# A four-layer scan and attention kernel: the program points at which transfers are issued are moved by a few tiles

## The chip, the cores and the metric

The kernel runs on one core of a Trainium2 chip. The metric is the device time of one launch in microseconds (us), as the median of repeated runs. A profile of one execution is shown beside it. Engines are written as in the profile: PE (matmul) and PEld (its weight loads), DVE (vector), ACT (scalar), POOL (GpSimd), and SP, the engine on which every transfer of this kernel is issued.

## The reference

The input is four images of 64 by 64 pixels and 96 channels. Layers 0 and 1 are state-space layers, layers 2 and 3 are attention without a softmax, each with a quantized feed-forward part:

```
x = x + ssm0(groupnorm(x));  x = x + ssm1(groupnorm(x))
t = tokens(x)
t = t + attn(ln(t));  t = t + ffn8(ln(t))        # layer 2, then the same for layer 3

ssm(x):   xi, z = split(x @ in_proj.T)                       # 192 channels each
          xc = silu(depthwise_conv3x3(xi) + b)
          for k in 0..3:                                     # four scan orders of the 4096 pixels
              dt, B, C = project(xc in order k);  delta = softplus(dt @ w + b)
              h[t] = exp(delta[t] * A) * h[t-1] + delta[t] * xc[t] * B[t]     # 16 states a channel
              y   += (sum over states of h[t] * C[t]) + D * xc,  put back in pixel order
          return (layernorm(y) * silu(z)) @ out_proj.T
```

In layer 0 the orders k = 1 and k = 3 run down the columns of the image. In layer 1 the orders run through windows of 2, 4 and 8 pixels.

## The kernel before, in words

Two images are worked on together: the 128 partitions hold 64 channels of each, and three groups j of 64 channels make the 192. Layers 0 and 1 with two pairs of images give four phases. A phase has 16 blocks, one for each order k and each quarter t of 1024 pixels, so there are 64 blocks. A block has 48 tiles: two halves g of the states, three channel groups j, eight states n. In all there are 3072 tiles, and the main loop walks over them with the index `i`. I call `i` modulo 48 the place in the block.

For tile i, POOL multiplies the state by C (`weigh`, L695). For the five states in `POOL_N` POOL also makes delta·x·B (`begin`, L652), and for the others PE spreads B (`row`, L662) and DVE multiplies (`product`, L676). ACT makes the decay (`decays`, L669), DVE scans (`scan`, L684), and PE sums over the states (`gather`, L727). `begin` runs two tiles ahead of the scan.

What a block needs is brought by transfers:

- The rows of B and C, spread over 64 partitions each, `brep` and `crep` (`rows_of` sets the tile, `spread`, L642, issues two transfers for a row). They share 11 buffers.
- Copies of delta and delta·x (`twice`, L592), four of each for every j, into 12 buffers `dup`. They run across the block boundary, up to place 55, that is place 7 of the next block.
- The next block's x (`load`, L529 and L532, places 1, 2 and 5 for k from 1 to 3), the partial result of this block (`recall`, L704, seven tiles ahead: places 41, 1 and 9), and the store of a finished partial result (`flush`, L744, places 34, 42 and 50, that is 2).
- B and C on their way through memory (`rows`, L555).

The convolution of the next pair (`conv_pieces`) and the closing part of the last pair (`tail_pieces`) are generators. They run in the background: the loop calls `advance()` once for a tile. Three things about it matter here. At 16 places of a block (`kept`: 17 to 32 if the next block has k = 0, else 13 to 28) it isn't called, since `prepare` uses the two `psM` buffers there. What a generator yields says whether it may be left at that point. At the first of the 16 places a generator that yielded something true is driven on within one tile until it yields False:

```
if place == kept[0]:
    while holds:
        advance()
```

A convolution unit (512 pixels) has 32 steps: one before and one after the normalization of its input, and for each j nine taps, each with two matmul calls (L289), and one for z (L299). A unit of the closing part (256 pixels) has 14: two with matmuls into `psM` (L360) and the statistics (L346 to L353), then variance, `normalize`, `back`, `scaled` (L392), two `gate` steps (L398), two output matmuls (L426 to L442), copies and stores.

The orders of PE, DVE, ACT and POOL are the order in which the program is written (`MANUAL`). SP isn't in that set: the framework's scheduler orders its transfers, by the order of writing and by when it believes that what they wait for is done. SP takes its transfers strictly one after the other, and a transfer that waits holds up those behind it.

After the 3072 tiles a planner (`run`) works off the two attention layers and the rest of the closing part.

Of the kernel before, what the change touches and what calls it, by code (L numbers as in the profile page):

```python
# [15 lines left out]
C = 96  # L16
# [6 lines left out]
T = 512  # L23
# [11 lines left out]
def kernel(ctx: ExitStack, tc: tile.TileContext, ins, out, layers=(0, 1, 2, 3)):  # L35
# [176 lines left out]
    def conv_pieces(w, xin, xc, zg, done):  # L212
# [8 lines left out]
        xbs = [part_of(n) for n in range(3)]  # L221
        yield False
        yield False
        for i in range(2):
# [35 lines left out]
        def load(t):  # L260
# [14 lines left out]
            return pads  # L275

        done.append(now[0])
        coming = load(0)
        for t in range(NT):
            pads, coming = coming, None  # L280
            yield False
            for i in range(2):
                nc.scalar.activation(pads[i][1], pads[i][1], AF.Identity, bias=norms[i][1], scale=norms[i][0])  # L283
            yield False
            for j in range(J):
                px = psM([128, T])
                for tap in range(9):
                    for i in range(2):
                        nc.tensor.matmul(  # L289
                            px[64 * i : 64 * i + 64], w["wf"][:, tap, 64 * j : 64 * j + 64],  # L290
                            pads[i][0][:, tap // 3 : tap // 3 + rows, tap % 3 : tap % 3 + HW],
                            start=(tap == 0), stop=(tap == 8),
                        )
                    yield MORE if tap < 8 else True
                xo = thin([128, T], "xo")
                nc.scalar.activation(xo, px, AF.Silu, bias=w["cb"][:, j, :])
                pz = psM([128, T])
                for i in range(2):
                    nc.tensor.matmul(  # L299
                        pz[64 * i : 64 * i + 64], w["wz"][:, 64 * j : 64 * j + 64],  # L300
                        pads[i][0][:, 1 : 1 + rows, 1 : 1 + HW], start=True, stop=True,
                    )
                zo = thin([128, T], "zo")
                nc.scalar.activation(zo, pz, AF.Silu)
                nc.sync.dma_start(xc[:, j, t * T : (t + 1) * T], xo)
                nc.sync.dma_start(zg[:, j, t * T : (t + 1) * T], zo)
                if j == J - 1 and t + 1 < NT:
                    coming = load(t + 1)
                if j == J - 1:
                    done[0] += 1  # L310
                yield False

    def tail_pieces(w, units, y, zg, xin, xout, tokens):
# [11 lines left out]
        for t in units:  # L325
            tt = slice(t * U, (t + 1) * U)
            if coming is None:
                while t * U >= flushed(y):
                    yield False
                coming = load(t)  # L330
                yield False
                yield False
            (yu, zu), coming = coming, None
            yt = wide([128, J, U], "yt")
            yt = yt.rearrange("p j (q c) -> p (j q c)", q=2).rearrange("p (q i j c) -> p q i j c", q=2, i=2, j=J)
            yn = yu.rearrange("p j c -> p (j c)").rearrange("p (q j i c) -> p q j i c", q=2, j=J, i=2)
            xr = st([C, 2, U], F32, "xr", 1)
            for i in range(2):
                nc.sync.dma_start(xr[:, i, :], xin[i][:, tt])

# [58 lines left out]

            normalize(0)  # L400
            yield False
            pn0 = back(0)
# [14 lines left out]
            if tokens:  # L417
# [12 lines left out]
                for i in range(2):  # L430
                    nc.scalar.copy(xo[:, i], pos[i][:, :, 0:C])
                    nc.sync.dma_start(xout[i][tt].rearrange("(q p) c -> p q c", p=128), xo[:, i])
                ready[0] = t + 1
            else:
# [9 lines left out]
                for i in range(2):  # L444
                    nc.scalar.copy(xo[:, i, :], pos[i])
                    nc.sync.dma_start(xout[i][:, tt], xo[:, i, :])
            yield False

# [52 lines left out]
    def prepare(ph, k, t):  # L501
# [47 lines left out]
        def rows(s):  # L549
            if s == 0:  # L550
                p["parts"] = st([96, TB], BF16, "spB", 2)
                p["bc"] = dr.tile([4 * N, TB], F32, tag="bc", name="bc", bufs=2)
            rests.append(thin([76, T], "proj"))
            nc.scalar.copy(rests[s], pps[s])
            nc.sync.dma_start(p["bc"][:, halves[s]], rests[s][0 : 4 * N])  # L555

# [44 lines left out]
        for j in range(J):  # L601
# [9 lines left out]
            at(base + 16 + (3 if k == 0 else 4) * j, inputs, j)  # L611
            copies = max(32 + 8 * j, base + 17)
            for m, key in enumerate(("deltas", "dus")):
# [3 lines left out]
        for s in range(2):  # L617
            at(base + 3 + s, rows, s)
            for q in range(3):
                at(base + 3 + 2 * q + s, cut, s, q)  # L620
# [5 lines left out]
    def rows_of(at, g):  # L626
# [3 lines left out]
        for n in range(g * GN, (g + 1) * GN):  # L630
            for v in (0, 1):
                if v or n in POOL_N:
                    out.append((first + n - g * GN - (7 if v else 9), at, v, n))
        return sorted(out)
# [97 lines left out]
    def flush(i):  # L732
# [9 lines left out]
        for src, dst in made[at]["views"]:  # L742
            nc.scalar.copy(src(yb), dst(py))  # L743
        nc.sync.dma_start(made[at]["img"](yd[ph][:, j, :]), yb)  # L744

# [268 lines left out]
    per = NG * J * GN  # L1014
    made, reps, sums, states, scanned, order = {}, {}, {}, {}, {}, [None]
    end = len(tiles)
    now, rest = [0], (L - TB) // 256
    with tc.manual_schedule(engines=MANUAL):
# [26 lines left out]
        rows = [row for at in range(len(blocks)) for g in range(NG) for row in rows_of(at, g)]  # L1045
        for i in range(-9, end + 4):
            while rows and rows[0][0] <= i:
# [164 lines left out]
```

## Time and profile before

| | |
|---|---|
| median of 3 runs | 11149.57 us (11146.85 to 11173.61) |
| the profiled execution's own time | 11149.85 us |
| its span, first to last instruction | 11148.1 us |
| POOL busy in the span | 10204.6 us (92%) |
| DVE busy in the span | 9926.4 us (89%) |
| multiplications by C (L695) | 3072 of 2354 ns, from 140.3 to 10545.8 us |
| transfers issued on SP's queue, share of 16 engines | 66.1% of the span |

An engine's busy time counts its own instructions, not its waits. A row of the profile gives the line, the engine, the operation, the output and inputs by name, the shapes, the count, the busy time, the mean of one in ns, and the idle time of the engine just before these instructions with what ended it. Block 13 is taken as an example later: its first multiplication L695 is number 624, at 2294.1 us, and block 14 begins at 2463.3 us.

### The profile page before, as it was taken

What the parts mean: (1) busy time and instruction counts of PE and PEld (TensorE: products, weight loads), DVE (VectorE), ACT (ScalarE), POOL (GpSimd) and SP (SyncE); (2) the same over time, 40 slices, a digit from 0 to 9 for tenths busy, and PEclk for the clock granted to TensorE, in tenths of its full rate; (3) what the DMA queues carried; (4) which work ended last, traced back from release to release, by engine and by line L of the source; (5) the groups of instructions that cost most, each with busy time, mean ns of one, the idle gap of its engine ahead of it and who ended that gap; (6) DMA issues with size and microseconds to landing.
All of it is one profiled execution on the core that took longest, in us unless ns stands there. A gap on an engine that the chain in (4) does not pass through costs nothing. (4 is left out here: it accounts for less than half of the span.)

```text
span 11148.1 us, 101994 instructions
## 1 busy us (share of the span) xinstructions
PE 8910.0 (80%) x30112; PEld 2880.5 (26%) x30112; DVE 9926.4 (89%) x6431; ACT 6423.1 (58%) x10575; POOL 10204.6 (92%) x5102
## 2 busy tenths in 40 slices
PE   7978888777777779887788878887778877778777
PEld 2222222111222212221222222222222322222365
DVE  3898999999999889989999999999999999999846
ACT  3656556554566646665566656665466655555576
POOL 3989999999999889999999999999999999999846
PEclk8989999888888889998888889998888888888877
DMA  5679976897578885798666656665556565556410
GB/s 134 158 141 162 141 160 157 145 134 136 149 171 151 140 151 149 157 159 132 138 169 157 157 146 169 164 159 143 149 157 156 155 149 148 143 137 159 122 33 22
DMA packets 1848188, 1604.57 MB, mean 144 GB/s; under 512 B 1412298, under 2 KB 1482892, under 8 KB 1847628
## 3 DMA queue, kind: packets, MB, share of 16 engines
q1 hardware_dynamic: 1847628, 1598.04, 66.1%
q8 instruction: 237, 3.88, 0.2%
q14 instruction: 323, 2.65, 0.1%
HBM read 1008.37 MB, written 186.65 MB: 107 GB/s over the span
## 5 line engine op out<-in xcount | busy, mean ns | idle before, releaser
L695 POOL TENSOR_TENSOR f<-f,crep 128x1024 f32<-128x1024 f32 x3072 | 7158.9, 2354 | 395.9 <-DVE f L684 296.6
L727 PE MATMUL psY<-f,fold 128*64 128x512 f32 x12288 | 3795.1, 698 | 183.4 <-POOL f L695 182.8
L684 DVE TENSOR_TENSOR_SCAN f<-f,state,psB 128x1024 f32<-128x1024 f32 x1584 | 3717.8, 2347 | 206.2 <-ACT f L669 50.1
L669 ACT ACTIVATE f<-delta,L_a 128x1024 f32<-128x1024 f32 x2112 | 2406.5, 1145 | 903.9 <-PE psY L727 829.8
L676 DVE TENSOR_TENSOR psB<-psB,du 128x1024 f32<-128x1024 f32 x2112 | 2558.9, 1212 | 362.9 <-PE psB L662 322.1
L662 PE MATMUL psB<-spB,sel 96*128 96x512 bf16 x4224 | 1387.8, 414 | 1613.5 <-DVE f L684 1599.0
L652 POOL TENSOR_TENSOR f<-du,brep 128x1024 f32<-128x1024 f32 x960 | 2265.7, 2360 | 127.2 <-PE psY L727 29.4
L684 DVE TENSOR_TENSOR_SCAN f<-psB,state,f 128x1024 f32<-128x1024 f32 x720 | 1676.7, 2329 | 76.8 <-POOL f L652 50.3
L727 PEld LDWEIGHTS psY<-f,fold 128*64 128x64 f32 x12288 | 974.9, 154 | 2525.3 <-issue 1806.8
L690 ACT COPY state<-f 128x1 f32<-128x1 f32 x2304 | 429.7, 188 | 2065.8 <-DVE f L684 2056.7
L669 ACT ACTIVATE psB<-delta,L_a 128x1024 f32<-128x1024 f32 x960 | 1070.2, 1115 | 696.0 <-DVE f L684 636.1
L684 DVE TENSOR_TENSOR_SCAN f<-f,psB 128x1024 f32<-128x1024 f32 x528 | 1208.3, 2288 | 57.6 <-ACT f L669 5.9
L662 PEld LDWEIGHTS <-sel 96*128 96x128 bf16 x4224 | 271.3, 99 | 3320.4 <-DVE f L684 2163.7
L289 PE MATMUL psM<-pad,wf 96*64 96x512 f32 x3456 | 901.4, 623 | 36.0 <-ACT pad L283 28.9
L684 DVE TENSOR_TENSOR_SCAN f<-psB,f 128x1024 f32<-128x1024 f32 x240 | 545.6, 2273 | 102.9 <-ACT psB L669 60.0
L718 PE MATMUL psY<-ysum,ident 128*128 128x512 f32 x768 | 554.5, 862 | 98.3 <-ACT ynew L743 86.7
L585 POOL TENSOR_TENSOR xs<-delta,xs 128x1024 f32<-128x1024 f32 x192 | 452.7, 2358 | 95.0 <-ACT delta L582 95.0
L569 PE MATMUL psM<-proj,dtw 12*128 12x512 f32 x768 | 455.2, 686 | 0.0
L543 PE MATMUL psM<-xs,xp 128*76 128x512 f32 x768 | 414.7, 651 | 5.5 <-DMA xs<-xcd 4.2
L718 PE MATMUL psY<-yold,ident 128*128 128x512 f32 (+2 forms) x960 | 370.6, 526 | 42.2 <-ACT ysum L739 26.7
L289 PEld LDWEIGHTS psM<-pad,wf 96*64 96x64 f32 x3456 | 221.4, 138 | 501.0 <-issue 422.6
L743 ACT COPY ynew<-psY 128x1024 f32<-128x1024 f32 (+2 forms) x312 | 242.4, 818 | 171.5 <-PE psY L727 171.5
(149 smaller groups left out, 6644.6 us busy)
## 6 DMA issues: line engine op xcount, KB each, us to landing
crep<-bc SPq DMA_DIRECT2D x2048, 256.0 KB, 4.8
delta<-delta SPq DMA_DIRECT2D x768, 256.0 KB, 4.8
du<-xs SPq DMA_DIRECT2D x768, 256.0 KB, 6.2
brep<-bc SPq DMA_DIRECT2D x640, 256.0 KB, 4.9
yd<-ynew SPq DMA_DIRECT2D x192, 512.0 KB, 7.8
xraw<-xcd SPq DMA_DIRECT2D x144, 512.0 KB, 8.5
yold<-yd SPq DMA_DIRECT2D x144, 512.0 KB, 8.9
xcd<-xo SPq DMA_DIRECT2D x96, 256.0 KB, 3.0
```

What stands on the lines that cost most here:

```text
L289: nc.tensor.matmul(px[64 * i : 64 * i + 64], w["wf"][:, tap, 64 * j : 64 * j + 64], pads[i][0][:, tap // 3 : tap // 3 + rows, tap % 3 : ta ...
L569: nc.tensor.matmul(pds[-1], order[0][1][64:76, j, :], rests[s][64:76], start=True, stop=True)
L585: nc.gpsimd.tensor_mul(xs[j], deltas[j], xs[j])
L652: nc.gpsimd.tensor_mul(f[:, 1:], made[at]["dus"][j][n % 2], reps[at, 0, n])
L662: nc.tensor.matmul(scanned[i][0][:, ss], sel[:, n, :], made[at]["parts"][:, ss], start=True, stop=True)
L669: nc.scalar.activation(out, made[at]["deltas"][j][n % 2], AF.Exp, scale=W[phases[ph][0]]["a"][:, k, j, n // 2 : n // 2 + 1])
L676: nc.vector.tensor_mul(scanned[i][0], scanned[i][0], made[at]["dus"][j][n % 2])
L684: nc.vector.tensor_tensor_scan(f[:, 1:], a, bu, 0.0 if t == 0 else states[at - 1][:, c : c + 1], ALU.mult, ALU.add)
L690: nc.scalar.copy(states[at][:, c : c + 1], f[:, TB : TB + 1])
L695: nc.gpsimd.tensor_mul(f[:, 0:TB], f[:, 1:], reps[at, 1, n])
L718: nc.tensor.matmul(o, of, v, start=(m % banks == 0), stop=False)
L727: nc.tensor.matmul(py[64 * e : 64 * e + 64, ss], fold, two[e][:, ss], start=False, stop=(n == g * GN + GN - 1),)
```

## The change

- `rows_of`: rows are issued seven (brep) and five (crep) tiles ahead of their first tile, where it was nine and seven.
- `prepare`: the copies `twice` begin at place 34 + 8j, where it was 32 + 8j (and not before base + 17). The transfer of B and C to memory becomes a step `spill` of its own, two tiles after `rows`.
- `flush` no longer stores: the store is kept and issued in `store`, two tiles later.
- `conv_pieces`: the stores of xo and zo are issued one step later (`away`), the step after z yields True instead of False, the load of the next input comes after the last stores, and four yields instead of two follow the first loads.
- `tail_pieces`: the first unit waits four yields instead of two after its load. The residual `xr` is loaded after `normalize(0)` instead of at the unit's start. Between the copies and the stores there is now a `yield True`, and the `yield False` at the unit's end is gone.

```
@@ conv_pieces
-        yield False
-        yield False
+        for _ in range(4):
+            yield False
...
+        outs = []
+        def away(j, t, xo, zo):
+            nc.sync.dma_start(xc[:, j, t * T : (t + 1) * T], xo)
+            nc.sync.dma_start(zg[:, j, t * T : (t + 1) * T], zo)
...
             for j in range(J):
+                if outs:
+                    away(*outs.pop())
                 px = psM([128, T])
...
-                nc.sync.dma_start(xc[:, j, t * T : (t + 1) * T], xo)
-                nc.sync.dma_start(zg[:, j, t * T : (t + 1) * T], zo)
-                if j == J - 1 and t + 1 < NT:
-                    coming = load(t + 1)
-                if j == J - 1:
-                    done[0] += 1
-                yield False
+                outs.append((j, t, xo, zo))
+                yield True
+            away(*outs.pop())
+            if t + 1 < NT:
+                coming = load(t + 1)
+            done[0] += 1
@@ tail_pieces
                 coming = load(t)
-                yield False
-                yield False
+                for _ in range(4):
+                    yield False
...
-            xr = st([C, 2, U], F32, "xr", 1)
-            for i in range(2):
-                nc.sync.dma_start(xr[:, i, :], xin[i][:, tt])
...
             normalize(0)
+            xr = st([C, 2, U], F32, "xr", 1)
+            for i in range(2):
+                nc.sync.dma_start(xr[:, i, :], xin[i][:, tt])
             yield False
...
                 for i in range(2):
                     nc.scalar.copy(xo[:, i], pos[i][:, :, 0:C])
+                yield True
+                for i in range(2):
                     nc.sync.dma_start(xout[i][tt].rearrange("(q p) c -> p q c", p=128), xo[:, i])
...
                 for i in range(2):
                     nc.scalar.copy(xo[:, i, :], pos[i])
+                yield True
+                for i in range(2):
                     nc.sync.dma_start(xout[i][:, tt], xo[:, i, :])
-            yield False
@@ prepare
             nc.scalar.copy(rests[s], pps[s])
+        def spill(s):
             nc.sync.dma_start(p["bc"][:, halves[s]], rests[s][0 : 4 * N])
...
-            copies = max(32 + 8 * j, base + 17)
+            copies = 34 + 8 * j
...
             at(base + 3 + s, rows, s)
+            at(base + 5 + s, spill, s)
@@ rows_of
-                    out.append((first + n - g * GN - (7 if v else 9), at, v, n))
+                    out.append((first + n - g * GN - (5 if v else 7), at, v, n))
@@ flush
-        nc.sync.dma_start(made[at]["img"](yd[ph][:, j, :]), yb)
+        stored[i] = made[at]["img"](yd[ph][:, j, :]), yb
+    def store(i):
+        if i in stored:
+            nc.sync.dma_start(*stored.pop(i))
@@ main loop
-        for i in range(-9, end + 4):
+        for i in range(-9, end + 6):
+            store(i - 5)
             while rows and rows[0][0] <= i:
                 spread(rows.pop(0))
```

More of the change, by code (lines that the diff above doesn't have):

```diff
@@ L1014 @@
     per = NG * J * GN
-    made, reps, sums, states, scanned, order = {}, {}, {}, {}, {}, [None]
+    made, reps, sums, states, scanned, stored, order = {}, {}, {}, {}, {}, {}, [None]
     end = len(tiles)
```

## The prediction

> **What bounds the kernel now.** I read the page's first row, then POOL's groups with their idle time, then SP's own waits, then SP and POOL around one block boundary, and ACT in one place where the background is driven on within a tile.
>
> ```profile
> PE 8910.0 (80%) x30112; PEld 2880.5 (26%) x30112; DVE 9926.4 (89%) x6431; ACT 6423.1 (58%) x10575; POOL 10204.6 (92%) x5102
> ```
> ```profile
> L695 POOL TENSOR_TENSOR f<-f,crep 128x1024 f32<-128x1024 f32 x3072 | 7158.9, 2354 | 395.9 <-DVE f L684 296.6 <-issue 61.0 <-POOL f L695 9.3
> L652 POOL TENSOR_TENSOR f<-du,brep 128x1024 f32<-128x1024 f32 x960 | 2265.7, 2360 | 127.2 <-PE psY L727 29.4 <-DMA du<-xs 20.9 <-DMA crep<-bc 20.5
> L585 POOL TENSOR_TENSOR xs<-delta,xs 128x1024 f32<-128x1024 f32 x192 | 452.7, 2358 | 95.0 <-ACT delta L582 95.0
> ```
>
> A block costs POOL 48 L695, 15 L652 and 3 L585, which is 66 × 2.36 = 155.5 us, and 64 blocks make 9950 us. The main loop runs from about 140 to 10548 us, so POOL bounds it. All of POOL's idle time there is some 570 us, and no better timing of transfers can win more. Of the waits in these rows only L652's carry a transfer's name, about 50 us. DVE is close behind: a tile costs it 2.34 for the scan and 11 times in 16 another 1.21, or 3.17 us against POOL's 3.24. So whatever stops DVE for more than a tile reaches POOL.
>
> ```profile
> SPq L642 <- POOL f L652: 1489.1, 252, 34.6
> SPq L592 <- ACT delta L582: 1168.3, 64, 34.7
> SPq L642 <- POOL f L695: 952.9, 746, 7.3
> SPq L305 <- ACT xo L296: 386.6, 57, 23.5
> ```
>
> SP waits much, but mostly because it is early: rows wait for one of their 11 buffers, and copies for softplus. A row goes out when the tile that frees its buffer, eight before its own first use, has been multiplied. The pair of crep issued at 2298.79 below is for tile 631, which POOL begins at 2318.84, 20 us later, against a median landing of 4.8 us.
>
> ```profile
> 2298.79 1.49 SPq L642 DMA_DIRECT2D crep<-bc  x2
> 2300.97 0.48 SPq L592 DMA_DIRECT2D delta<-delta  x1
> 2302.09 0.37 SPq L704 DMA_DIRECT2D yold<-yd  x1
> 2303.38 10.17 SPq L592 DMA_DIRECT2D delta<-delta  x1
> 2313.60 0.59 SPq L532 DMA_DIRECT2D xraw<-xcd  x1
> 2314.28 7.24 SPq L744 DMA_DIRECT2D yd<-ynew  x1
> 2321.57 5.82 SPq L592 DMA_DIRECT2D delta<-delta  x1
> ...
> 2334.84 1.05 SPq L532 DMA_DIRECT2D xraw<-xcd  x1
> 2335.94 7.60 SPq L592 DMA_DIRECT2D du<-xs  x2
> 2343.64 0.55 SPq L704 DMA_DIRECT2D yold<-yd  x1
> ```
> ```profile
> 2348.32 2.36 POOL L652 TENSOR_TENSOR f<-du,brep 128x1024 f32<-128x1024 f32 x1 [4.45 <-DMA du<-xs]
> ```
>
> These are places 0 to 9 of block 13 (layer 0, k = 3). Transfers of image columns (yold, xraw, yd) cost SP nothing themselves, but the next issue then takes 6 to 10 us instead of 0.6. Here the queue is full, and the order in it decides. The last du copies arrive 4.45 us late.
>
> ```profile
> 8838.04 1.34 ACT L392 ACTIVATE psM<-psM,L_lnb,L_lnw 128x128 f32<-128x128 f32 x3
> 8841.05 0.32 ACT L431 COPY xn<-psM 128x192 f32<-128x192 f32 x1 [1.67 <-PE psM L428]
> 8845.11 0.32 ACT L431 COPY xn<-psM 128x192 f32<-128x192 f32 x1 [3.74 <-PE psM L428]
> ```
>
> This is block 53, place 13: six held steps of the closing part in one tile. ACT stands 5.4 us in its queue for PE, and decays that DVE needs wait behind it.
>
> **The change part by part.**
>
> *Held steps of the closing part.* Before, a unit ends in a False, so at most seven steps follow in one tile. Now the True before the stores runs into the next unit's two True steps, and after `back(0)` ten steps follow. Walking the 14 steps through the 32 free places of a block gives, for each of the tails run in phases 1 to 3, bursts of 3, 6 and 6 steps before (in the phase's blocks 0, 2, 5) and of 8, 10, 10, 10 and 10 after (0, 1, 2, 4, 5). Block 62 has 7 before and 10 after. That is 16 long bursts. The added steps are six matmul calls L360 (1.7 us) and both statistics on ACT, which take 2.0 us each in the timeline (3000.22 to 3002.26, 3003.51 to 3005.54). About 5 us are added to a chain in which ACT already comes last. Bounds: 0, if POOL's lead over what follows hides all, and 5. I take 3.5, since six-step bursts cost POOL 0 to 3 us at present and so have used that lead. 16 × 3.5 = 56, and six more bursts of the present kind at 1 us: +60.
>
> *Held steps of the convolution.* The step after z now yields True, so a unit cannot be left between its j. Bursts were up to 8 steps. Walking the 32 steps gives 28 steps with 24 taps at block 23 and at block 39 (place 13), 27 steps with 23 taps at block 0, place 17 (7 before), and 9 taps instead of 3 at block 3. The later blocks fall into step, one unit for 32 places, and have none. A tap is 901.4 us of busy L289 / 864 = 1.04 us on PE, with `row` and `gather` of the next tiles queued behind it. PE runs about two tiles (6 us) ahead: 2 × (25 - 6) = 38, block 0: 16 taps more and 2 fewer just before it, 15, block 3: 6, and 4 to 6 us back from short bursts that vanish: +55. Bounds: 30, if PE's cover is twice that, and 85.
>
> *Rows, copies and store, away from column transfers.* A row's buffer comes free as before, and the five tiles still give 17 us against landings of 4.8 (median) and 9.5 (longest). Copies come two tiles later, with 14 to 36 us from the last issue to its use in blocks without column transfers. The `spill` has 20 tiles. The store keeps its `part` buffer two tiles (7 us) longer, and the next taker is 14 places on. 0. What hides these is SP's lead. Without it each row group would lose its lateness, which is the third rival.
>
> *The same beside column transfers.* Recalls (places 1, 9) and xraw (1, 2, 5) stay while rows and copies fall back two places. The row of tile 7 (place 0, now 2) goes behind the recall and the first xraw. It would be issued by 2318 instead of 2300 (10.17 + 7.24 us of blocked issues ahead) and land near 2325, while POOL wants it at 2318.84: about 6 us. The last du copy (place 7, now 9) falls behind the recall at 9, 7.6 us by the row above, and stays late by what it was plus 1 or 2. Together 7 to 8 us a block. Of 12 blocks with both kinds, 7 have under 6 us between the last du issue and its use, the others 11 to 14: 7 × 7 + 5 × 1, or +55. Bounds: -15 (the store, now behind an xraw, frees ACT's L538, which waits 29 us for xraw by name) and +110.
>
> Two rules of the Trainium skill bear on this. The page "DMA: Bandwidth & Descriptors", section "Rules for kernel authors", says to issue a transfer early and wait late, which speaks against the whole change. Read as a price it would charge every row two tiles less cover. The trace gives rows 20 us at a landing of 4.8, so I charge only where the queue is full: 55, not 128 row groups × 6.8 = 870. Its section "Anatomy of one DMA" fits 2.0 us + bytes/436e3 (for another queue), an estimate of 3.2 us for the 512 KB recall. By that the two recalls and xraw would be hidden and this part would be 0. The trace has a median landing of 8.5 us and blocked issues of 6 to 10, and I use those.
>
> *The tail within those blocks.* In phase 1 the bursts at blocks 20 and 21 load yu in the burst itself and use it in the same tile, behind a full queue. PE's wait for yu there is 10 to 12 us in three cases today. The residual xr now has two tiles instead of ten. Two bursts × 10 for this, and 10 for yu loads at place 1 of the two blocks, less 10 now lost in block 22: +20 (bounds 0, 45).
>
> *What it saves.* The first yu gets two more tiles: POOL lost 8.0 and 7.7 us in blocks 16 and 32 (L372 waiting for ACT): -13. Pads are mostly loaded before the 16 free places instead of two steps ahead (ACT L283 waits 28 + 19 us for them, of which some 25 reach POOL), though unit 1 of the last two convolutions has one step less: -25. First xb: -5. SP's 387 us at L305 release nothing that POOL waits for: 0.
>
> *The end.* After the loop about as many units are left, in a slightly changed order: 0 (-15 to +15).
>
> Sum: 60 + 55 + 0 + 55 + 20 - 43 = +147 us on the profiled execution's own 11149.85 (span 11148.1 and 1.75 around it), so 11297. That execution lies 0.3 us from the median, so I say 11295.
>
> **The rivals.**
>
> *Faster: SP really was in the way.* Every transfer that POOL, DVE, ACT or PE waits for by name today comes in time, and the bursts hide behind POOL. By name POOL waits about 70 us for transfers, ACT 61 for xraw and its like (L538), PE 54 for yu. With half of the others reaching POOL, -100: 11050. For it: the SP waits above. Against it: they are buffer waits, which do not end sooner when the row is asked for later. It decides if the bursts cost under 40 us and the column blocks get faster. Chance 0.12.
>
> *Hidden.* Costs and savings cancel: the bursts are absorbed, the order at the column blocks is rearranged by the scheduler. 11150, chance 0.09.
>
> *Rows become the bound.* If SP reaches rows late because stores and copies now stand just before them, each of 128 row groups waits about 3 us: +384 on top of little else, 11530. Against it: landed rows lie 9 us or more ahead even in block 13. Chance 0.07.
>
> *As summed*, 11295, chance 0.72, its own range 11200 to 11390.
>
> **How the numbers follow.** A difference of 0.3% (33 us) is about what a measurement of this kernel can tell. Faster by more: the first rival and a sliver, 0.12. Within: 0.09. Slower: 0.79. The range reaches into the first rival, and upward to the upper bounds of held steps and column blocks taken together (147 + 30 + 55 + 25 less a part that overlaps): 11100 to 11410. Left out are most of the row rival and half of the faster one.
>
> **What would show it.** If right: POOL's idle before L695 grows from 396 to about 500 us, and a crep wait appears among its releasers (2.9 us today) at place 7 of layer 0's blocks 5, 6, 13 and 14. In blocks 23 and 39 PE runs taps L289 for some 25 us without a gap, with DVE idle inside. ACT waits for PE at L431, L445 and L346 grow, and L283's for pads shrink. In all other blocks nothing changes: SP still waits for POOL before rows, about 20 us ahead. It is wrong if POOL's idle time falls in layer 0's blocks with k = 1 and 3, if the bursts leave no mark on DVE, or if rows are late in layer 1.

## The result, and the profile after

The changed kernel takes 11446.07 us (median of 4 runs, 11424.07 to 11465.47) against 11152.74 of the kernel before beside it. The ratio is 1.0259, with an interval of 1.0236 to 1.0282. From here on a ratio is also given in us, as the ratio less one times 11150; this one is +289 us. The direction was forecast, at half the size: +147 was predicted, and 11446 lies above the range.

The first row and the multiplication rows of the page after. Lines have moved: `weigh` is L708 now, `begin` L665, `product` L689.

```profile
PE 9070.8 (79%) x30112; PEld 2925.3 (26%) x30112; DVE 9927.6 (87%) x6431; ACT 6419.0 (56%) x10561; POOL 10207.5 (89%) x5102
```
```profile
L708 POOL TENSOR_TENSOR f<-f,crep 128x1024 f32<-128x1024 f32 x3072 | 7162.4, 2356 | 638.3 <-DVE f L697 526.5
...
L689 DVE TENSOR_TENSOR psB<-psB,du 128x1024 f32<-128x1024 f32 x2112 | 2558.7, 1211 | 484.2 <-PE psB L675 435.1
...
L665 POOL TENSOR_TENSOR f<-du,brep 128x1024 f32<-128x1024 f32 x960 | 2267.4, 2362 | 184.6 <-PE psY L740 50.5
```

POOL and DVE are busy for as long as before (10204.6 and 9926.4 us there): what is new on them is idle time. POOL's idle time ahead of the multiplication by C grew from 395.9 to 638.3 us, and what ended 526.5 of it is DVE's scan (296.6 before). DVE in turn waits 435.1 us for PE's `row` (L675; 322.1 before), and its scans wait 260 us for ACT's decays (142 before). For transfers POOL waits, by name, about 25 us more than before. So most of the loss is not POOL waiting for a transfer. It starts in PE and ACT and passes through DVE. PE's busy time did change: the same 30112 matmuls take 9070.8 us, where it was 8910.0, and the mean granted clock of PE is 0.858 instead of 0.870. This returns below. The profiled execution of after took 11465.47 us, 19 above its median, so differences of the two profiles come out somewhat larger than 289.

SP's own waits, the first rows (line, engine and line waited for, us in total, times, longest):

```profile
SPq L655 <- POOL f L665: 1320.8, 239, 40.1
SPq L604 <- ACT delta L594: 1122.1, 64, 33.5
SPq L655 <- POOL f L708: 1037.5, 737, 10.8
SPq L280 <- ACT xo L304: 361.9, 68, 21.4
```

The waits that the change was aimed at are about as long as before (1489.1, 1168.3, 952.9 and 386.6).

Where the time lies: I took the starts of the 3072 multiplications in both traces and the differences block by block. The main loop takes 308 us more and the end 11.6. The four phases lose 47, 105, 79 and 77 us. In phases 1 to 3 it is the first seven blocks, in which the closing part runs, that lose most (103, 52 and 61 us), and blocks 23 and 39, of the convolution, lose 15 each. By place in the block POOL's idle time grew by 99 us at place 16 and 56 at place 20, and at no other place by more than 29.

I call the steps that are driven on within one tile a burst. One long burst of the closing part in the kernel after: block 36, place 13. The timeline gives start, duration, engine, line, operation, and in brackets the idle time ahead and what ended it. PE first:

```profile
6299.30 0.67 PE L449 MATMUL psM<-xr,ident 96*96 96x256 f32 x2 [2.40 <-DVE zu L402]
6300.57 2.82 PE L451 MATMUL psM<-zu,ow 64*96 64x256 f32 x6 [0.60 <-DVE zu L402]
6303.32 1.17 PE L449 MATMUL psM<-xr,ident 96*96 96x256 f32 x2
6304.42 2.87 PE L451 MATMUL psM<-zu,ow 64*96 64x256 f32 x6
6307.22 2.93 PE L364 MATMUL psM<-ident,yu 128*128 128x128 f32 x12
6309.94 1.06 PE L675 MATMUL psB<-spB,sel 96*128 96x512 bf16 x2
```
```profile
6303.43 0.37 ACT L454 COPY xn<-psM 96x256 f32<-96x256 f32 x1 [3.50 <-PE psM L451]
6307.33 0.37 ACT L454 COPY xn<-psM 96x256 f32<-96x256 f32 x1 [3.53 <-PE psM L451]
6308.91 0.33 ACT L350 ACTIVATE yt<-psM 128x192 f32<-128x192 f32 x1 [1.21 <-PE psM L364]
...
6313.92 1.14 ACT L682 ACTIVATE f<-delta,L_a 128x1024 f32<-128x1024 f32 x1
```
```profile
6311.04 1.23 DVE L689 TENSOR_TENSOR psB<-psB,du 128x1024 f32<-128x1024 f32 x1 [6.14 <-PE psB L675]
6315.09 2.29 DVE L697 TENSOR_TENSOR_SCAN f<-f,psB 128x1024 f32<-128x1024 f32 x1 [2.82 <-ACT f L682]
```
```profile
6317.45 4.67 POOL L708 TENSOR_TENSOR f<-f,crep 128x1024 f32<-128x1024 f32 x2 [7.72 <-DVE f L697]
```

Up to 6307 this is the unit's own end, as before: output matmuls (L449, L451) and their copies (L454). Then the next unit follows without a break: PE's two calls L364, and ACT's statistics from 6308.91 to 6312.8. PE's `row` for the next tile (L675) stands behind L364, and ACT's decay (L682) behind the statistics. DVE gets them one after the other, waits 6.14 us for the row and then 2.82 for the decay, and POOL stands 7.72 us. The scan begins when the decay is there; its product has been ready since 6312.27, so here the decay alone sets the length of the stall.

PE's matmuls in this burst run at half speed: the clock granted to PE from 6303 to 6310 is 0.50. How much that matters can be read from block 34, where the kernel after and the kernel with the changed closing part alone (the second experiment below, in which L364 is L357 and `weigh` is L698) run the same ten steps. The end of the burst and POOL's stall behind it, in the kernel after (granted clock 1.00 from 5986 to 5992) and in the other (0.50 from 5924 to 5930):

```profile
5988.70 1.53 PE L451 MATMUL psM<-zu,ow 64*96 64x256 f32 x6
5990.16 1.60 PE L364 MATMUL psM<-ident,yu 128*128 128x128 f32 x12
5999.68 2.36 POOL L708 TENSOR_TENSOR f<-f,crep 128x1024 f32<-128x1024 f32 x1 [4.92 <-DVE f L697]
```
```profile
5924.22 2.87 PE L444 MATMUL psM<-zu,ow 64*96 64x256 f32 x6
5927.02 2.93 PE L357 MATMUL psM<-ident,yu 128*128 128x128 f32 x12
5937.25 2.35 POOL L698 TENSOR_TENSOR f<-f,crep 128x1024 f32<-128x1024 f32 x1 [7.29 <-DVE f L687]
```

The same pair in block 17 gives 4.9 and 8.7 us. In the kernel after, L364 runs at clock 1.00 in six of the 16 long bursts (blocks 16, 17, 32, 33, 34 and 48) and POOL stands 4.3 to 5.1 us just behind them; in the other ten it runs at 0.50 to 0.54, and POOL stands 5.7 to 8.1 us, and some 14 in blocks 20 and 21, where a transfer is late as well. Why the clock is lower in the one and not in the other, no run shows.

### The profile page after: what moved, and what is told of

Same layout as the page of the kernel before. It is cut to its first block, busy times and chain, and to the rows that moved or that the text cites. A ratio compares the mean times of both kernels' runs of the same rounds, so it can differ in the third digit from the quotient of the medians.

```text
span 11463.7 us, 102259 instructions
## 1 busy us (share of the span) xinstructions
PE 9070.8 (79%) x30112; PEld 2925.3 (26%) x30112; DVE 9927.6 (87%) x6431; ACT 6419.0 (56%) x10561; POOL 10207.5 (89%) x5102
## 5 line engine op out<-in xcount | busy, mean ns | idle before, releaser
L708 POOL TENSOR_TENSOR f<-f,crep 128x1024 f32<-128x1024 f32 x3072 | 7162.4, 2356 | 638.3 <-DVE f L697 526.5
L740 PE MATMUL psY<-f,fold 128*64 128x512 f32 x12288 | 3888.8, 710 | 205.5 <-POOL f L708 205.1
L689 DVE TENSOR_TENSOR psB<-psB,du 128x1024 f32<-128x1024 f32 x2112 | 2558.7, 1211 | 484.2 <-PE psB L675 435.1
L682 ACT ACTIVATE f<-delta,L_a 128x1024 f32<-128x1024 f32 x2112 | 2406.2, 1145 | 912.1 <-PE psY L740 841.5
L675 PE MATMUL psB<-spB,sel 96*128 96x512 bf16 x4224 | 1401.8, 418 | 1654.9 <-DVE f L697 1636.9
L665 POOL TENSOR_TENSOR f<-du,brep 128x1024 f32<-128x1024 f32 x960 | 2267.4, 2362 | 184.6 <-PE psY L740 50.5
L740 PEld LDWEIGHTS psY<-f,fold 128*64 128x64 f32 x12288 | 990.3, 156 | 2605.5 <-issue 1832.4
L682 ACT ACTIVATE psB<-delta,L_a 128x1024 f32<-128x1024 f32 x960 | 1070.2, 1115 | 615.0 <-DVE f L697 558.3
L675 PEld LDWEIGHTS <-sel 96*128 96x128 bf16 x4224 | 274.4, 100 | 3396.7 <-DVE f L697 2207.5
L297 PE MATMUL psM<-pad,wf 96*64 96x512 f32 x3456 | 942.8, 636 | 69.2 <-ACT pad L289 54.4
L731 PE MATMUL psY<-ysum,ident 128*128 128x512 f32 x768 | 529.8, 828 | 69.3 <-ACT ynew L756 67.3
L588 ACT ACTIVATE delta<-psM,L_dtb 128x512 f32<-128x512 f32 x384 | 260.9, 680 | 72.0 <-PE psM L581 71.6
```

The source lines that it names most:

```text
L297: nc.tensor.matmul(px[64 * i : 64 * i + 64], w["wf"][:, tap, 64 * j : 64 * j + 64], pads[i][0][:, tap // 3 : tap // 3 + rows, tap % 3 : ta ...
L665: nc.gpsimd.tensor_mul(f[:, 1:], made[at]["dus"][j][n % 2], reps[at, 0, n])
L675: nc.tensor.matmul(scanned[i][0][:, ss], sel[:, n, :], made[at]["parts"][:, ss], start=True, stop=True)
L682: nc.scalar.activation(out, made[at]["deltas"][j][n % 2], AF.Exp, scale=W[phases[ph][0]]["a"][:, k, j, n // 2 : n // 2 + 1])
L689: nc.vector.tensor_mul(scanned[i][0], scanned[i][0], made[at]["dus"][j][n % 2])
L708: nc.gpsimd.tensor_mul(f[:, 0:TB], f[:, 1:], reps[at, 1, n])
```

## The experiments

Each kernel was timed beside the kernel before. A part "alone" is that part of the change put into the kernel before.

**Transfers alone.** Rows two tiles later, copies at 34 + 8j, `spill`, and the store two tiles later.

```
-            copies = max(32 + 8 * j, base + 17)
+            copies = 34 + 8 * j
...
-                    out.append((first + n - g * GN - (7 if v else 9), at, v, n))
+                    out.append((first + n - g * GN - (5 if v else 7), at, v, n))
```

> Rows, copies, spill and store moved as in the change; both background generators as before. If held steps of the background made the change slow, this alone is within 30 us of the kernel before (a few us lost at places 7 and 15 of layer 0's column blocks). If the order on SP made it slow (rows and copies late), it is slower by 150 to 300 us.

1.0071 (1.0056 to 1.0086), +79 us, between the two cases that were expected. In the profile layer 0's two phases lose 50 and 41 us, those of layer 1 4 each. POOL's idle time at place 15 grew by 59 us and at place 7 by 20. The stall at place 15 is 9 to 12 us in exactly the seven blocks that the prediction counted (5, 6, 13, 14, 21, 29, 30), where it was 6.0 at most. Those blocks take 38 us more. A good part of the rest lies where column transfers begin: 7.0 and 6.5 us in blocks 3 and 4, 5.3 and 6.2 in 19 and 20. In the whole change the stall is as long in blocks 13, 14 and 30 (9.0 to 9.4 us), but 6.5 in block 21 and 3.6 or less in 5, 6 and 29. In block 13, SP and POOL of the kernel after:

```profile
2367.29 7.28 SPq L604 DMA_DIRECT2D du<-xs  x3
2374.67 1.38 SPq L717 DMA_DIRECT2D yold<-yd  x1
2376.10 6.57 SPq L604 DMA_DIRECT2D du<-xs  x1
```
```profile
2386.58 2.36 POOL L665 TENSOR_TENSOR f<-du,brep 128x1024 f32<-128x1024 f32 x1 [9.04 <-DMA du<-xs]
```

The last copy of delta times x now comes after the recall (yold), whose transfer of image columns fills the queue: the copy's issue is held 6.57 us, and POOL waits 9.04 us instead of 4.45.

**The closing part alone.** Four yields after the first load, residual after `normalize(0)`, stores a step later, no False at the unit's end.

```
+                yield True
+                for i in range(2):
                     nc.sync.dma_start(xout[i][:, tt], xo[:, i, :])
-            yield False
```

> Only the closing part's generator as in the change. If held steps are the cause: 16 runs of 8 to 10 steps within one tile at about 10 us of POOL idle each, and some more in the two column blocks, so 170 to 230 us slower. If the transfers of the main loop are the cause: within 40 us of before.

1.0191 (1.0175 to 1.0207), +213 us. Blocks 16 to 22 take 1.5, 16, 15, 5, 15, 21 and 23 us more, and the same blocks of the next phases 5.5, 12, 9, -2, 8, 12, 18.5 and 5, 12.5, 9, 8, 14, 14, -1. This is nearly the whole of what the changed kernel loses there.

**The convolution alone.** The stores a step later, True instead of False after z, four yields at its start.

```
+                if outs:
+                    away(*outs.pop())
...
-                yield False
+                outs.append((j, t, xo, zo))
+                yield True
```

> Only the convolution's generator as in the change. Without the changed closing part the units fall differently: by walking the steps, runs of 27, 29, 27 and 29 steps in blocks 24, 26, 40 and 42 and of 27 in block 0. If a held run of some 24 taps costs POOL 20 us as in the changed kernel: 4 x 20 + 17 - 25 for pads, 60 to 90 us slower. If PE's lead hides them: within 30 us.

1.0089 (1.0072 to 1.0106), +99 us. Without the other parts the long runs fall into blocks 24, 26, 40 and 42, and these take 24.5, 25.5, 21.2 and 24.4 us more; block 0 takes 15.6. These are runs of 23 to 25 us on PE, each with a stall of POOL of 19 to 21 us at place 16.

**The closing part with its False.** As the closing part alone, but a unit again ends in a False, after the stores.

```
                 for i in range(2):
                     nc.sync.dma_start(xout[i][:, tt], xo[:, i, :])
+            yield False
```

> The closing part's generator as in the change, but with a yield False after the stores (a 15th step), so that a held run ends with the unit. By walking the steps: runs of 6, 1, 8 and 1 steps in each tail instead of 8, 10, 10, 10 and 10. If the run across the unit's end is the cause, most of e2's loss is gone: 0 to 50 us slower than before. If the late loads of the residual and of yu are the cause, it is as slow as e2 (these loads stand as in the change).

1.0051 (1.0036 to 1.0066), +57 us, of which the end has 30 (one step more in a unit leaves one unit more for it). So 213 - 57 = 156 us hang on this one False. Blocks 16 to 22 now differ by -3, 2, -1, 5, 0, 7 and -4 us from before. The bursts that remain (by the walk 6 and 8 steps, none of which reaches into the next unit) are nearly free, but for block 21, where PE waits 11.4 us for a late residual. With a step more in each unit the units also fall elsewhere, and there are fewer bursts. Block 37 has one in both kernels: POOL stands 0.8 us behind the eight steps here, and 7.8 behind the ten of the closing part alone. What costs is what follows without the False: the two steps with L364 and the statistics.

**Transfers and recalls.** As the transfers alone, with the recall five tiles ahead instead of seven, so that it again stands behind the copies.

```
-            if 0 <= i + 7 < end and tiles[i + 7][1] == 0 and tiles[i + 7][3] == 0:
-                recall(i + 7)
+            if 0 <= i + 5 < end and tiles[i + 5][1] == 0 and tiles[i + 5][3] == 0:
+                recall(i + 5)
```

> e1 (rows, copies, spill and store moved) with the recalls moved by the same two tiles (five ahead instead of seven: places 43, 3 and 11), so that rows and copies stand before them in the queue again. If the order against the column transfers costs e1 its 79 us, most of it comes back: 0 to 30 us slower than the kernel before, and the idle time at places 7 and 15 of the column blocks falls back. If rows and copies are late in themselves, it stays 60 to 90 us slower.

1.0048 (1.0032 to 1.0065), +54 us, 25 less than the transfers alone and more than the 0 to 30 that order by itself should leave. By place, against those: place 15 -50 us and place 7 -9, but place 13 +31 and place 14 +11. The copies come sooner (by name POOL waits 34.5 us for du, and 79.3 with the transfers alone), and now the recall is late (PE waits for yold up to 8.7 us).

**Recalls alone.** The same edit in the kernel before.

> The kernel before with the recalls alone two tiles later. If what POOL waits for in the column blocks is the queue's order, the last du copies come sooner there (4 to 6 us idle at place 15 in seven blocks at present): 15 to 40 us faster. If the queue's order does not matter: the same within 10 us, or slower if the recalled partial results themselves are late.

1.0069 (1.0051 to 1.0088), +77 us, where a gain was expected if the order in the queue was what mattered. The stalls for du at place 15 went (-21 us), and place 13 took 81 us more. One row of the waits, by engine and line:

```profile
PE psY L718 <- DMA yold<-yd: 101.5, 12, 12.4
```

PE waits up to 12.4 us for the recalled partial result. Seven tiles ahead was not early at all where image columns are in the queue.

**After, with room kept for a burst.** A unit of the closing part does not start `back(0)` when fewer than 11 free places are left before the kept ones. (`gap` yields a false value that carries a number of steps.)

```
-            yield False
+            yield gap(11)
...
-                if aside is not None and not (plan and place in kept):
+                room = kept[0] - place if place < kept[0] else per - place + 13
+                if aside is not None and not (plan and place in kept) and getattr(holds, "steps", 0) <= room:
```

> The changed kernel, in which a unit of the closing part does not begin its held steps (at back(0)) when fewer than 11 places are left before the 16 kept ones. All else stands. If the long runs within a tile cost what e2 says, it is 100 to 170 us faster than the changed kernel (some 1.1 to 1.6% slower than before, with e1's 79 us and the convolution's runs left). If late loads (xr, yu) or the order of steps cost it, less than 40 us faster than the changed kernel.

1.0253 (1.0232 to 1.0274), +282 us: next to nothing won, where 100 to 170 were expected if the long bursts were all that costs. Against after, blocks 16 to 23 gain 120 us, 32 to 39 78 and 48 to 53 59. Blocks 24 to 28 lose 125 and 40 to 44 96, and the end 23. Places left empty push the convolution back, which then has to catch up with two steps in a tile and with long runs in blocks 26 to 28 and 42 to 44 (stalls of 12 to 27 us at place 16).

**Before, with room kept.** The same in the kernel before with 8 places, and four yields for the first load.

> The kernel before with the same rule (8 places for its shorter run) and with four yields instead of two after a tail's first load. If held runs cost in the kernel before too (runs of 6, 6 and 3 steps, some 25 us of POOL idle by the trace) and the first yu is late by two tiles (13 us): 15 to 40 us faster. If the places that are left empty cost more: the same or up to 30 us slower.

1.0094 (1.0075 to 1.0112), +105 us, where 15 to 40 us faster or at most 30 slower was expected. The units now all start at the same places, and stalls of 2 to 4 us come at places 2 and 38 of the closing part's blocks (+63 and +53 us in all); the convolution is late in blocks 24, 27, 29 and 40 by some 20 us each. The bursts of the kernel before were the cheaper way.

**Copies earlier.** The kernel before with its copies two places earlier, the opposite of the change.

```
-            copies = max(32 + 8 * j, base + 17)
+            copies = max(30 + 8 * j, base + 17)
```

> The kernel before with one edit: the copies of delta and delta x are put two places earlier (30 + 8j and not before base + 17), the mirror of what the change does to them. Theory A, order in a full queue: in layer 0's blocks with both kinds of column transfers the last du copy (place 7, now 5) then stands ahead of the third xraw and the recall at 9, its stall of about 4.5 us at place 15 (7 blocks) goes, and little else takes its place, since what falls behind are xraw loads, which the kernel uses much later: 15 to 40 us faster. Theory B, no order of these transfers is better than the one before: whatever falls behind is late, by the pattern of the recall put later, and the time stays within 15 us or grows. Seen in: L652 waits for du<-xs (20.9 us before), and in ACT's L538 wait for xraw.

1.0023 (1.0016 to 1.0031), +26 us. POOL's stalls for du at place 15 are gone (place 15 -20 us), but ACT, which needs xraw, waits:

```profile
ACT xs L538 <- DMA xraw<-xcd: 68.8, 17, 7.0
```

It was 28.8 us in 8 waits before. Places 9 and 10 take 32 us more; ACT's decays stand behind L538 in its order, which would explain it. So neither order is free in these blocks: what is put behind is late.

**First yu alone.** The kernel before, with four yields instead of two after the first load of a closing part.

```
-                yield False
-                yield False
+                for _ in range(4):
+                    yield False
```

> The kernel before with one edit: the first unit of each closing part waits four steps instead of two after its load, as in the change. This is the saving that the prediction put at -13 us (stalls of 8 us in blocks 16 and 32). But the two more steps shift the later units by two places of the 32, so other steps come to stand at the boundary of the 16 places. By the walk of the steps the bursts stay at six steps or less. Theory A, as predicted: 8 to 20 us faster, seen in blocks 16 and 32 alone. Theory B, the shift costs as much elsewhere: within 8 us of before, with blocks 17 to 22 each changed by some us of both signs.

0.9992 (0.9986 to 0.9999), -9 us. Blocks 16 and 32 gain 5.9 and 3.5 us. This is the one edit of the change that was found to help, and it helps less than a measurement of three runs can tell.

**After with the False.** The kernel after with the False at the unit's end back, and nothing else.

> The kernel after with one edit: the step that ends a unit of the closing part yields False again, after the stores. No other step moves. Theory A, the run across the unit's end is the largest single cost in the whole change as it was in the closing part alone (156 of 213 us there): the long bursts at blocks 16 to 22, 32 to 38 and 48 to 53 shrink to those of the closing part with False, and the kernel is 110 to 170 us faster than after, that is 1.011 to 1.016 of before. Theory B, the bursts only bring to light a delay that another part would cause in the same tiles (the copies at place 15 and 16): under 60 us is won, ratio over 1.020.

1.0171 (1.0154 to 1.0187), +191 us, 98 less than after; between the two expectations. Blocks 16 to 23 gain 111 us, 32 to 39 80, but blocks 24 to 27 and 40 to 43 lose 70 and 56: with a step more in each unit the convolution begins elsewhere in the block, and has three long runs in each of these phases (16, 20 and 24 taps, in blocks 24, 25, 27 and 40, 41, 43). The closing part's share is thus about as large as in the closing part alone, and a part of it goes back to the convolution.

**After with the old convolution.**

```
-                outs.append((j, t, xo, zo))
-                yield True
+                nc.sync.dma_start(xc[:, j, t * T : (t + 1) * T], xo)
+                nc.sync.dma_start(zg[:, j, t * T : (t + 1) * T], zo)
...
+                yield False
```

> The kernel after with the convolution's part undone (its stores at once, False after each z, the next load at once, two steps after the first load); transfers and closing part stay as changed. The three parts alone cost 79, 213 and 99 us, 391 together, and the whole change 289. Theory A, the difference is the convolution's: in the whole change it falls into step with two long runs (blocks 23 and 39, 15 us each) and block 0 (20) where alone it has four of some 24: about 50 us faster than after, ratio near 1.021. Theory B, it is the overlap of the closing part's bursts with the late column transfers in the same tiles of blocks 16 to 22: then this kernel is well under 79 + 213 = 292 above before, at 190 to 220, and the convolution's whole 70 to 99 us come off, ratio 1.017 to 1.0195.

1.0241 (1.0223 to 1.0260), +269 us. Transfers and closing part alone add up to 79 + 213 = 292; the 23 us of overlap are within the intervals. Next to them the convolution's part costs only 20 us, less than either theory said, and by the intervals anything from nothing to some 50. In the profile blocks 0, 23 and 39 gain 15, 18 and 22 us over after, as the first theory said, and blocks 2 to 7 lose 24 net. ACT's waits for pads are 39 us here and 24 in after, a saving of the convolution's part that goes with it.

**Bursts over two tiles.** The kernel after; up to five of the steps that must follow are issued in the last tile ahead of the kept places.

```
+                if plan and place == kept[0] - 1:
+                    for _ in range(5):
+                        if holds:
+                            advance()
```

> The kernel after with one edit: in the last tile before the 16 kept places, up to five of the steps that must follow are issued already there, the rest at the first kept place as ever. The same steps are done by the end of that place; no later step moves. Theory A, length in one tile is the price (PE's row and ACT's decay stand behind the whole burst, and cover is two tiles): ten steps become five and five, each near the bursts of before, and of some 10 us for each of 16 bursts more than half goes: 70 to 130 us faster than after, ratio 1.014 to 1.019. Theory B, the price is the waits inside (yu or xr late, PE and ACT in turn), whichever tile they fall in: within 35 us of after, ratio 1.022 to 1.027, with the idle time moved from places 12 and 13 on to the tile ahead.

1.0255 (1.0241 to 1.0269), +284 us, as after. The steps did go into two tiles. In block 36, PE and ACT:

```profile
6307.33 2.77 PE L451 MATMUL psM<-zu,ow 64*96 64x256 f32 x6 [0.60 <-DVE zu L402]
6310.02 3.68 PE L740 MATMUL psY<-f,fold 128*64 128x512 f32 x8
...
6314.55 1.53 PE L451 MATMUL psM<-zu,ow 64*96 64x256 f32 x6
6316.01 1.60 PE L364 MATMUL psM<-ident,yu 128*128 128x128 f32 x12
```
```profile
6309.60 1.11 ACT L682 ACTIVATE psB<-delta,L_a 128x1024 f32<-128x1024 f32 x1
6310.65 0.36 ACT L454 COPY xn<-psM 96x256 f32<-96x256 f32 x1
6316.12 0.37 ACT L454 COPY xn<-psM 96x256 f32<-96x256 f32 x1 [5.11 <-PE psM L451]
```

A decay (L682) and a `gather` (L740, 3.68 us) now stand between the halves, so PE's own work for the main loop takes most of the tile that was gained. The decay behind the statistics comes 9.0 us after the start of place 14, where it came 11.1, and POOL's stall at place 16 is 5.6 us instead of 7.7. PE's clock has a part in this: it is 1.00 for L364 here, which takes 1.60 us instead of 2.93. Elsewhere that is given back: over all blocks places 16 and 20 win 21 and 13 us, and places 18, 15, 13 and 17 lose 23, 13, 7 and 7. By its size this is the second theory's case, but the idle time did not move to the tile ahead: splitting the work once does not make room for it on PE and ACT.

**The same in the kernel before**, with three steps and the first-yu edit.

> The kernel before with two edits: the first unit of the closing part waits four steps instead of two, and bursts are split over two tiles in the same way (up to three steps in the last tile before the kept places). Theory A: bursts of six at two blocks of each closing part and the convolution's short ones cost some us each, 5 to 10 bursts a phase, and lose half: 15 to 45 us faster than before. Theory B, bursts of six are within the cover, and there is nothing to win but the first yu's 9 us: within 15 us of before.

0.9992 (0.9983 to 1.0000), -9 us, what the first-yu edit gives alone. Bursts of six steps had nothing to give back. No version here beats the kernel before by more than these 9 us.

## Why the prediction came to half of the loss

Its sum by parts, and what each part measured:

| part of the sum | forecast | measured |
|---|---|---|
| rows, copies, spill, store (0 + 55) | +55 | +79 (alone) |
| closing part (60 + 20, first yu -13) | +67 | +213 (alone) |
| convolution (55, pads -25, xb -5) | +25 | +20 (whole change less that without it), +99 alone |
| overlap | none | -23 |
| sum | +147 | +289 |

**Which engine, which way: right.** POOL stays the bound, its busy time is the same, SP's waits before rows release nothing, rows are not late in layer 1 (4 us a phase). The first rival, that SP was in the way, and the third, that rows become the bound, are both out.

**Held steps of the closing part: the step that failed.** "About 5 us are added to a chain in which ACT already comes last", and of those 3.5 reach POOL. The walk found the right blocks, and ACT's chain did get about that much longer: from the end of the unit's last copy to the end of the statistics it is 6307.7 to 6312.8, or 5.1 us, in block 36. But the False costs 156 us, 9.8 us for each of the 16 long bursts, where 3.5 were put. At the two places behind each of these bursts where POOL stalls (16 and 17, or 20 and 21) it stands 139 us with the closing part alone and 17 with its False: 7.7 us a burst. The remaining 34 us lie elsewhere and are not split further.

Two things were wrong in the term. First, I let the cover of six-step bursts serve again: they cost "0 to 3 us at present and so have used that lead", I wrote, and still took 1.5 of the 5 away. Splitting the six-step bursts wins nothing, and blocks that went from no burst to ten steps (17, 20, 33, 36, 49, 52) lose as much with the closing part alone, 13 us on average, as those that went from six to ten (18, 21, 34, 37, 50, 53), also 13. So six steps fit, and what comes on top arrives in full: the stall is 4.3 to 5.1 us at clock 1.00, near the 5 that were added. Second, I took PE's clock as full. The six calls L364 were put at 1.7 us, which is what they take at clock 1.00 (1.60); in ten of the 16 bursts of the kernel after they take 2.84 to 2.93 at about half of it, the output matmuls ahead of them slow down too, and ACT waits for both. In the pairs of blocks 34 and 17 this added 2.4 and 3.8 us to the stall. With the closing part alone, L364 ran at 0.50 to 0.57 in twelve of the 16 bursts; at about 3 us for each I estimate the clock at some 36 of the 156 us. No run changed the clock alone. The upper bound of 5 us for a burst was therefore no bound. Late transfers in blocks 20 and 21 come on top (next paragraph).

**The tail beside column transfers: right in kind.** The term was 20. The residual xr is late in blocks 20 and 21 in the kernel after (PE waits 8.6 and 16.0 us for it by name). Not foreseen were the convolution's first inputs: DVE waits 11.5 us for xb in block 22, behind xraw, du and yold in the queue. How much of the 57 us that are left with the False is this and how much the end, the runs do not separate further.

**Beside column transfers: right place, 55 against 79, and partly by luck.** Seven blocks were counted, and with the transfers alone all seven have the stall. But its parts were the other way round. The row of tile 7 was put at 6 us a block, and POOL's wait at place 7 grew by 2.3 on average; the last du copy was put at 1 or 2 us more, and the stall at place 15 grew by 7.6. These seven blocks lose 38 us, not 49, and some 40 are lost in blocks that were put at 1 us or nothing. The -15 of the lower bound, that the store behind an xraw would free ACT's L538, did not come: ACT waits for transfers there about 75 us where it waited 61 (by name, at L548 and L538).

**Convolution.** Blocks 23 and 39 were right, with the long runs in place. In block 23 PE and POOL of the kernel after:

```profile
4155.96 5.32 PE L297 MATMUL psM<-pad,wf 96*64 96x512 f32 x24
4161.11 1.03 PE L307 MATMUL psM<-pad,wz 96*64 96x512 f32 x4
4163.40 7.95 PE L297 MATMUL psM<-pad,wf 96*64 96x512 f32 x36 [1.26 <-ACT xo L304]
4171.17 1.03 PE L307 MATMUL psM<-pad,wz 96*64 96x512 f32 x4
4172.18 7.95 PE L297 MATMUL psM<-pad,wf 96*64 96x512 f32 x36
4179.96 1.03 PE L307 MATMUL psM<-pad,wz 96*64 96x512 f32 x4
4180.92 0.61 PE L675 MATMUL psB<-spB,sel 96*128 96x512 bf16 x2
```
```profile
4187.56 4.66 POOL L708 TENSOR_TENSOR f<-f,crep 128x1024 f32<-128x1024 f32 x2 [21.36 <-DVE f L697]
```

The run is 25 us, the stall 21.36, against 25 and 19 in the prediction. The blocks lose only 15 because smaller stalls of before are gone. Block 0 was put at 15 and lost 19.

**Savings.** First yu 9 instead of 13. ACT's waits for pads fell from 28 + 19 to 17 + 7 us, which cannot give the 25 us at POOL that were entered. The end was put at 0 and lost 11.6.

## What to carry to other kernels

Work that is put behind an engine in order costs by what of it exceeds the cover, and cover that a first burst uses is not there for the next: count it once, and price PE's part at the clock that the trace grants there (1.60 or 2.93 us here for the same twelve matmuls). Where a yield or a barrier separates two runs of held work, taking it away joins them, and that can cost more than all the transfers that it was to ease (156 us against 79). A wait on a queue is no cost as long as nobody waits for what comes out of it, and in the full queue of these blocks each kind of transfer that was put later was the next one to be late.

## What was not expected of the hardware

In layer 0's column blocks every order that was tried had a late transfer: du by 9 to 12 us (transfers later), yold by up to 12.4 (recalls later), xraw by up to 7.0 (copies earlier). The order before was the best of the five that ran, and each shift of two tiles cost 26 to 79 us. I had read the recall, seven tiles ahead, as early and safe to move.

PE's granted clock decides a good part of what a burst costs. The same ten steps ran at 1.00 in one kernel and at 0.50 in another, with POOL's stall at 4.92 and 7.29 us. The mean over the run says little about it: the closing part with its False has a mean of 0.860, nearly that of the kernel after (0.858), and loses 57 us where that loses 289.
